# Depthwise products of eight channels at four shifts, side by side in the array

## The chip, the cores and the metric

The kernel runs on one NeuronCore of a Trainium2 chip. The metric is the device time of one execution in microseconds; the median of several runs is compared.

## The reference

The input x is 32 images of 96 channels of 56 x 56 pixels in float32. Two residual layers follow one another, each on a group-normalised copy of its input.

```python
# layer 0: weights and activations quantised to 4 bits
y = act_q(bn1(conv1x1(gn(x), qw(w1))))        # 96 -> 576 channels
y = act_q(bn2(conv3x3_depthwise(y, qw(w2))))  # 576 channels, each alone
x = x + bn3(conv1x1(y, qw(w3)))               # 576 -> 96 channels
# layer 1: three branches of 32 channels, then a 3x3 convolution
n = gn(x)
a = gated_conv3x3(n[:, :32])
b = abs(inverse_fractional_fourier(gated_mix(fractional_fourier(n[:, 32:64]))))
c = inverse_fft(gated_mix(fft(n[:, 64:])))
x = x + conv3x3(concat(a, b, c))
```

## The kernel before

**Layer 0.** The 576 hidden channels are cut into five blocks of 128 (the last has 64). Pixels are handled by parity: u = 0 to 3 numbers the four combinations of odd and even row and column, so an image of a channel is four images of 28 x 28. `expand(b, u)` forms a block's hidden channels at one parity with float matmuls into a pair of PSUM banks (`pe`, L689); `quant_act` (L636, L638) applies scale and ReLU on ScalarE and cuts to 4 bits on VectorE, into `q1s`, whose rows of 872 bytes hold a 28 x 28 image with margins (PQ = 30 bytes a row, QS = 872).

The depthwise convolution needs a channel's four parities in different partitions. The data therefore go through DRAM: `leave(b, u)` writes `q1s` to `sd`, and `enter(b, h)` reads 64 channels back into a tile `d` of two groups, each with 32 channels x 4 parities in the 128 partitions. `depthwise(b, g)` then forms all four output parities of 32 channels at once. A 3 x 3 window on parity images is four shifts (0 or 1 row, 0 or 1 column), so each half image takes four accumulating matmuls of 128 rows by 128 columns, and a group eight, into a PSUM pair `pd` (L723). `quant_act` follows, into `q2s`. There are 18 groups an image. `leave2` and `enter2` take the result through `gd` in DRAM into `q2`, where channels are partitions again, and `project(u)` (`pp`, L748) ends the layer.

**Layer 1.** It has many small steps: transposes (L1031), transforms (L937, L948, L964, L975, L1042), spatial products (`spatial`, L1088), channel mixes in 32-column matmuls of which four write to the four 32-partition strips of one bank (`mix_f`, L1009, and `mix_t`, L1072), and the last 3 x 3 convolution (`final`, L1145), split by a Winograd transform (L1119, L1122). Its tiles have one buffer each. L825 and L843 normalise its input.

**Order.** Three streams (normalising and splitting an image, the rest of layer 0, layer 1) are merged by `arrange`, which also releases the transfers, all issued by SP. Then the class `Order` takes every instruction of the program and plans it anew: `needs` finds what each must wait for, `model` gives each a duration and a lag, `pack` is a list scheduler, run forward and backward eight times, and `hold` fixes the planned order on each engine. The model prices an 8-bit matmul of 392 columns at cols / 2350, that is 0.167 us. It counts no cost for a change of the array's form. Only matmuls with at most 64 input rows are kept together by `group`, which the depthwise ones, with 128 rows, are not.

**Set-up.** The depthwise weights are built on the chip: for each of the 18 groups, VectorE multiplies the quantised taps with a block-diagonal pattern into `dw` (L502).

## Time and profile before

| quantity | value |
|---|---|
| median of 3 runs | 3622.18 us (3622.07 to 3627.27) |
| profiled execution, its own time | 3621.32 us |
| its span, first to last instruction | 3619.5 us |
| granted TensorE clock, mean | 0.947 |
| DMA traffic | 406.08 MB, 491611 packets |

The profile is one execution; the share of an engine's busy time is over the span. The difference of 1.8 us between time and span lies around the first and last instruction. A float32 matmul leaves two records in the trace, an 8-bit one leaves one. Records of matmuls overlap[...], so their mean duration is longer than the distance from one to the next.

### The profile page before, as it was taken

To read this page: it belongs to the slowest core of one execution; us is meant where nothing else is said; L and a number is where in the kernel's file an instruction comes from. 1 tells how busy PE (TensorE), PEld (TensorE's weight loads), DVE (VectorE), ACT (ScalarE), POOL (GpSimd) and SP (SyncE) were. 2 spreads that over 40 slices of the span, in tenths; PEclk is the share of its full clock that TensorE was granted. 3 is DMA by queue.
4 is the path that set the end of the run, shared out by engine and by line. 5 is a ranking of instruction groups with operands and counts; after the bars stand their busy time and mean duration, and the time that the engine had idled before them with its cause. 6 is when DMAs were issued, how large, how long until landed. Compare 5 with 4: busy or idle time off the path is not lost. (4 is left out here: it accounts for less than half of the span.)

```text
span 3619.5 us, 50492 instructions
## 1 busy us (share of the span) xinstructions
PE 3326.5 (92%) x17024; PEld 2059.6 (57%) x17024; DVE 2458.2 (68%) x5553; ACT 2109.3 (58%) x2792; POOL 584.3 (16%) x657
## 2 busy tenths in 40 slices
PE   3799999999999999999999999999999999999987
PEld 2555565556565555565555565555655555655554
DVE  6457676667667667667676766676676676766765
ACT  3566555566556566555566656566555665555542
POOL 3111110111101111101111101111101111101100
PEclk9899999999999999999999999999999999999997
DMA  4344444444454444444444444444444444444332
GB/s 109 103 120 120 113 121 112 108 123 113 116 123 112 106 124 112 115 123 103 108 124 114 118 122 103 114 123 113 117 123 102 118 119 110 124 112 107 101 91 48
DMA packets 491611, 406.08 MB, mean 112 GB/s; under 512 B 221094, under 2 KB 443288, under 8 KB 490328
## 3 DMA queue, kind: packets, MB, share of 16 engines
q1 hardware_dynamic: 487168, 400.10, 44.1%
q10 hardware_dynamic: 4184, 2.75, 0.3%
q8 instruction: 135, 2.21, 0.3%
q14 instruction: 124, 1.02, 0.1%
HBM read 202.71 MB, written 199.97 MB: 111 GB/s over the span
## 5 line engine op out<-in xcount | busy, mean ns | idle before, releaser
L723 PE MATMUL pd<-d,dw 128*128 128x392 fp8e4 x4608 | 1026.7, 358 | 62.8 <-DMA d<-sd 60.3
L636 ACT ACTIVATE q2s<-pd,o,s 128x784 uint8<-128x784 f32 x576 | 578.3, 1004 | 628.8 <-PE pd L723 620.2
L1145 PE MATMUL pc<-V,wcw 96*96 96x392 f32 x2304 | 887.3, 495 | 9.3 <-DVE V L1122 9.3
L636 ACT ACTIVATE q1s<-pe,o,s 128x784 uint8<-128x784 f32 (+1 forms) x640 | 628.9, 1003 | 285.1 <-PE pe L689 283.0
L723 PEld LDWEIGHTS <-dw 128*128 128x128 fp8e4 x4608 | 468.2, 104 | 551.5 <-issue 276.8
L689 PE MATMUL pe<-hi,w1r 96*128 96x392 f32 x1280 | 526.2, 415 | 97.8 <-ACT q1s L636 70.8
L1145 PEld LDWEIGHTS pc<-V,wcw 96*96 96x96 f32 x2304 | 374.7, 164 | 213.6 <-issue 173.2
L689 PE MATMUL pe<-lo,w1r 96*128 96x392 f32 x1280 | 471.1, 368 | 3.3 <-POOL lo L680 2.9
L638 DVE TENSOR_SCALAR q1s<-q1s 128x218 uint32<-128x218 uint32 (+1 forms) x640 | 232.5, 371 | 257.5 <-ACT q1s L636 252.1
L689 PEld LDWEIGHTS pe<-hi,w1r 96*128 96x128 f32 x1280 | 243.0, 192 | 237.9 <-ACT q1s L636 141.0
L638 DVE TENSOR_SCALAR q2s<-q2s 128x196 uint32<-128x196 uint32 x576 | 150.3, 273 | 238.0 <-ACT q2s L636 227.4
L680 POOL TENSOR_TENSOR lo<-v,hi 96x784 fp32r<-96x784 f32 x128 | 238.2, 1861 | 258.0 <-ACT hi L679 241.2
L689 PEld LDWEIGHTS pe<-lo,w1r 96*128 96x128 f32 x1280 | 246.7, 193 | 52.0 <-issue 16.8
L748 PE MATMUL pp<-q,w3q 128*96 128x392 fp8e4 x1280 | 244.0, 333 | 18.9 <-DMA q<-gd 8.3
L628 POOL TENSOR_TENSOR stb<-veb,mhalf 96x1 f32<-96x1 f32 x32 | 23.2, 726 | 1324.2 <-DVE veb L627 1324.2
L748 PEld LDWEIGHTS <-w3q 128*96 128x96 fp8e4 x1280 | 151.1, 124 | 107.5 <-issue 41.5
L679 ACT CAST hi<-v 96x784 fp32r<-96x784 f32 x128 | 107.7, 841 | 174.0 <-DVE v L676 173.3
L758 DVE SCALAR_TENSOR_TENSOR x<-pp,s,x 96x392 f32<-96x392 f32 x256 | 145.4, 617 | 72.9 <-PE pp L748 70.8
L1022 POOL COPY cat<-sq 32x392 f32<-32x392 f32 x256 | 144.9, 566 | 287.2 <-ACT sq L1018 278.7
L1088 PE MATMUL ps<-s,g 128*128 128x392 f32 x512 | 187.7, 502 | 0.0
L1102 ACT ACTIVATE cat<-ps,b 32x392 f32<-32x392 f32 x256 | 162.5, 636 | 16.3 <-PE ps L1088 12.1
L676 DVE TENSOR_SCALAR v<-x,sta 96x784 f32<-96x784 f32 x128 | 89.6, 700 | 101.3 <-POOL lo L680 79.9
(158 smaller groups left out, 4393.5 us busy)
## 6 DMA issues: line engine op xcount, KB each, us to landing
d<-sd SPq DMA_DIRECT2D x288, 218.0 KB
gd<-q2s SPq DMA_DIRECT2D x576, 98.0 KB
sd<-q1s SPq DMA_DIRECT2D x512, 109.0 KB
q<-gd SPq DMA_DIRECT2D x128, 392.0 KB
x<-in_x_dram SPq DMA_DIRECT2D x384, 98.0 KB
out_dram<-x SPq DMA_DIRECT2D x384, 98.0 KB
pd<-pq SPq DMA_DIRECT2D x32, 808.5 KB
F<-pd SPq DMA_DIRECT2D x64, 392.0 KB
```

The lines of the kernel that those rows point to most:

```text
L636: nc.scalar.activation(dst, ps, AF.Relu, bias=offset, scale=scale)
L638: nc.vector.tensor_scalar(w, w, 4, 0x0F0F0F0F, ALU.logical_shift_right, ALU.bitwise_and)
L679: nc.scalar.copy(s["hi"][:, u, :], v)
L680: nc.gpsimd.tensor_tensor(s["lo"][:, u, :], v, s["hi"][:, u, :].bitcast(F32), ALU.subtract)
L689: nc.tensor.matmul(ps[:, half, :HN], w1[:, 128 * b : 128 * (b + 1)], part[:, u, HN * half : HN * (half + 1)], start=(n == 0), stop=(n == 1),)
L723: nc.tensor.matmul(ps[:, half, :HN], dw[n][:, t, :], view(s["d"][b, g], PQ * (14 * half + t // 2) + t % 2, [[PQ, 14], [1, HH]]), start=(t ...
L748: nc.tensor.matmul(ps[:C, half, :HN], w3[:, b * C : (b + 1) * C], q2[b][:, u, HN * half : HN * (half + 1)], start=(b == 0), stop=(b == NB ...
L758: nc.vector.scalar_tensor_tensor(part, src, A3, part, ALU.mult, ALU.add)
L1022: nc.gpsimd.tensor_copy(cat[G : 2 * G, r : r + 7, 1 : 1 + W], src)
L1088: nc.tensor.matmul(ps[:, :HN], s["g0"][:, 128 * t : 128 * (t + 1)], view(s0, PQ * (14 * half + t // 2) + t % 2, [[PQ, 14], [1, HH]]), star ...
L1102: nc.scalar.activation(dst, src, AF.Identity, bias=b0[2 * G : C], scale=1.0)
L1145: nc.tensor.matmul(ps[:C, :HN], wc[:, k, C * dx : C * (dx + 1)], V[:, :, dx : dx + W], start=(dx == 0), stop=(dx == 2),)
```

## The change

The partitions of a depthwise matmul now hold 8 channels x 4 parities x 4 shifts instead of 32 channels x 4 parities. All taps of an output then lie in one matmul of 128 rows by 32 columns, and nothing accumulates. A group of 32 channels is four such sets of 8; set t writes PSUM partitions 32t to 32t + 31. A group still has eight matmuls of 392 columns.

The tile `d` now has each image four times, once for each shift. `enter` issues two DMAs, one for each row shift; each fills every second partition with runs of 6,944 bytes (eight groups of 8 channels in one run), and the two column shifts are source rows that overlap all but one byte. The layouts of `sd` and `gd` in DRAM and the order of channels in the host's constants change to suit. Weights shrink from [128, 4, 128] to [128, 4, 32] a group; `d` grows from [128, 2, 872] in a pool of three buffers to [128, 8, 872] in a new pool, p4, of two. The planner's DMA model is replaced by one that counts packets and run lengths, and a matmul of 32 weight columns is priced at 0.055 us.

```diff
-                        elif pool in ("p1", "p3"):
+                        elif pool in ("p1", "p3", "p4"):
...
-                move = size / 200e3
                 for a in (outs[0], ins[0]):
...
+                    run = min(run, n * size / 16)
+                    n *= size / run
+                    move = max(move, n * 0.0017 if run < 512 else math.ceil(n / 16) * max(0.05 + run / 43e3, run / 27e3))
...
                     took = max(cols / 2350.0, 0.05)
+                    if weights == G and cols >= HN:
+                        took = 0.055
...
-            d = cp.tile([128, 4, 128], FP8, tag=f"dw{g}", name=f"dw{g}")
+            d = cp.tile([128, 4, 32], FP8, tag=f"dw{g}", name=f"dw{g}")
             nc.vector.tensor_tensor(
-                view(d.rearrange("p s m -> p (s m)"), 0, [[128, 4], [4, 32], [1, 4]]),
-                view(w2, 16 * g, [[4, 4], [0, 32], [1, 4]]),
-                view(eye, 0, [[0, 4], [1, 32], [0, 4]]),
+                view(d.rearrange("p s m -> p (s m)"), 0, [[32, 4], [4, 8], [1, 4]]),
+                view(w2, 16 * g, [[4, 4], [0, 8], [1, 4]]),
+                view(eye, 0, [[0, 4], [1, 8], [0, 4]]),
...
+    p4 = Pool(ctx.enter_context(tc.tile_pool(name="p4", bufs=2)), "p4", 2, tiles)
...
-                s["sd", b] = dp.tile([n, 32, 4, QS], FP8, tag=f"sd{n}", name=f"sd{i}_{b}")
+                s["sd", b] = dp.tile([4, 8, 4 * n, QS], FP8, tag=f"sd{n}", name=f"sd{i}_{b}")
             q = q1s[(NB * i + b) % 2]
-            nc.sync.dma_start(out=s["sd", b][:, :, u, :].rearrange("g c n -> c g n"), in_=q[: blk(b), u, :])
+            nc.sync.dma_start(out=s["sd", b][u], in_=q[: blk(b), u, :])
...
-            d = p3.tile([128, 2, QS], FP8, tag="d", name=f"d{i}_{b}_{h}")
-            src = s["sd", b][2 * h : 2 * h + 2].rearrange("g c u n -> (c u) g n")
-            nc.sync.dma_start(out=d, in_=src)
+            d = p4.tile([128, 8, QS], FP8, tag="d", name=f"d{i}_{b}_{h}")
+            n = 8 * QS - 32
+            src = s["sd", b][:, :, 8 * h : 8 * (h + 1), :].rearrange("u c g n -> (u c) (g n)")[:, :n]
+            flat = d.rearrange("p g n -> p (g n)")[:, :n]
+            (pitch, _), row = flat.ap
+            for y in range(2):
+                part = bass.AP(src.tensor, src.offset + PQ * y, [list(src.ap[0]), [1, 2], [1, n]])
+                dst = bass.AP(flat.tensor, flat.offset + pitch * y, [[2 * pitch, 64], list(row)])
+                nc.sync.dma_start(out=dst, in_=part)
             for g in range(2):
-                s["d"][b, 2 * h + g] = d[:, g, :]
+                s["d"][b, 2 * h + g] = d[:, 4 * g : 4 * g + 4, :]
...
                     nc.tensor.matmul(
-                        ps[:, half, :HN],
+                        ps[32 * t : 32 * (t + 1), half, :HN],
                         dw[n][:, t, :],
-                        view(s["d"][b, g], PQ * (14 * half + t // 2) + t % 2, [[PQ, 14], [1, HH]]),
-                        start=(t == 0),
-                        stop=(t == 3),
+                        view(s["d"][b, g][:, t, :], PQ * 14 * half, [[PQ, 14], [1, HH]]),
+                        start=True,
+                        stop=True,
...
-                s["gd", b] = dp.tile([32, n, 4, 2 * HN], FP8, tag=f"gd{n}", name=f"gd{i}_{b}")
-            nc.sync.dma_start(out=s["gd", b][:, g], in_=s["q", b, g])
+                s["gd", b] = dp.tile([n, 32, 4, 2 * HN], FP8, tag=f"gd{n}", name=f"gd{i}_{b}")
+            nc.sync.dma_start(out=s["gd", b][g], in_=s["q", b, g])
```

## The prediction

> **What bounds the kernel now.** I read the page's busy times first, then the busy times of a steady stretch, then the groups of instructions, then the matmuls in order of time, and last the DMA rows.

> ```profile
> PE 3326.5 (92%) x17024; PEld 2059.6 (57%) x17024; DVE 2458.2 (68%) x5553; ACT 2109.3 (58%) x2792; POOL 584.3 (16%) x657
> L723 PE MATMUL pd<-d,dw 128*128 128x392 fp8e4 x4608 | 1026.7, 358 | 62.8 <-DMA d<-sd 60.3
> L636 ACT ACTIVATE q2s<-pd,o,s 128x784 uint8<-128x784 f32 x576 | 578.3, 1004 | 628.8 <-PE pd L723 620.2
> ```

> TensorE is the bound: 92% busy, and the depthwise products (L723) are its largest group. ScalarE, which empties their PSUM, stood idle 620 us waiting for them. The steady stretch says the same more sharply:

> ```profile
> 500.00:3000.00 2500.00, 2356.93 (x12149) 1458.09 (x12148) 1729.20 (x3910) 1504.77 (x1992) 401.81 (x459) 0.95 0.46 116
> ```

> TensorE (first number after the length) 94.3%, VectorE 69%, ScalarE 60%, DMA engines 46%. The period of an image comes from one instruction that runs once in each, layer 1's L843:

> ```profile
> L843 DVE TENSOR_SCALAR torus<-x,stb x32: 1895/1900/1901, 144.3 to 3527.0; 32x3136 f32<-32x3136 f32 x32
> ```

> (3527.0 - 144.3) / 31 = 109.1 us. In it TensorE works 102.9 us, VectorE 75.5, ScalarE 65.7. Now matmuls in order of time (start, us, count):

> ```profile
> 1303.31 0.34 PE L689 MATMUL pe<-hi,w1r 96*128 96x392 f32 x1
> 1303.49 0.34 PE L689 MATMUL pe<-lo,w1r 96*128 96x392 f32 x1
> 1303.76 1.51 PE L1009 MATMUL pz<-F,g 98*32 98x392 f32 x12
> ...
> 3469.92 4.12 PE L1088 MATMUL ps<-s,g 128*128 128x392 f32 x12
> ...
> 3480.39 2.85 PE L1009 MATMUL pz<-F,g 98*32 98x392 f32 x32
> 3484.31 2.92 PE L723 MATMUL pd<-d,dw 128*128 128x392 fp8e4 x16 [1.08 <-DMA d<-sd]
> ```

> Three readings. A depthwise matmul follows the last by (2.92 - 0.34) / 15 = 0.172 us; I use 0.171. The full-width float matmul of 392 columns (L1088) comes every 0.33 us, the 32-column one (L1009), four side by side in 32-row strips of PSUM, every (2.85 - 0.49) / 31 = 0.076: the array already overlaps them fourfold. And entering that form costs: L1009 starts 0.27 us after an L689 that is normally followed after 0.18. Over all such places the trace gives 270 against 176 ns going in, 422 against 328 coming out: **94 ns a switch, 188 ns a visit.**

> ```profile
> q1 hardware_dynamic: 487168, 400.10, 44.1%
> ...
> d<-sd SPq DMA_DIRECT2D x288, 218.0 KB
> ...
> PE pd L723 <- DMA d<-sd: 60.3, 33, 3.2
> ```

> The images come in 288 transfers; one wait an image, 1.8 us on average, reaches TensorE.

> [...]

> **The change, part by part.**

> *Depthwise matmuls.* Removed: 4608 x 0.171 = 788 us of TensorE. Added: the same count, four to a slot of 0.171 if they stand together, and 0.188 for each uninterrupted run of them among full-width work. So run lengths decide. The trace before has 907 runs: 242 single, 259 of two, 89 of three, 57 of four, 88 of five, 30 of six, 97 of sixteen, 32 of thirty-two, 13 others. Three prices:
> - the same runs: each ceil(m/4) x 0.171 + 0.188, together 439 us, saving 349. The runs over eight save 316 of it, the short ones 33: a single costs 0.359 instead of 0.171, a pair is even;
> - the same runs, but no matmul with its weight load under 0.055 (the planner's figure; the smallest ones of the trace, L1031, come every 0.054 to 0.059): 475, saving 313;
> - all in eights: 576 x (0.342 + 0.188) = 305, saving 483.

> I take 400. The planner's ranks space depthwise matmuls closer when each is priced 0.055 instead of 0.167, so more of them fit between two final matmuls (L1145, which stands just before 464 of the 907 runs).

> *Filling.* TensorE then needs 102.9 - 400/32 = 90.4 us an image. At 94.3% that is a period of 95.9. I take 92%, hence 98.3, because a group takes TensorE about 0.5 us and ScalarE still 1.00: while layer 1 waits for its own DMAs, layer 0 now runs at ScalarE's pace and TensorE has gaps. VectorE would be at 77%, ScalarE at 67%; neither sets the end. Gain 31 x 10.8 = 335 us.

> *Images fetched four times.* 288 transfers of 256 packets of 872 bytes become 576 of 64 packets of 6,944. Recorded packets: 872 bytes 51 ns on average, 3,136 194, 7,392 370 (median 285), 12,544 966. The new size by the median 268 ns, by the mean 348, by the slowest row 535. Then 36864 x 0.348 / 16 = 802 us of all 16 engines against 235: DMA share from 44% to (1596 + 567) / 3280 = 66%; ends 61% and 79%. One pair of fetches: 8 packets an engine, 2.8 us instead of 16 x 0.051 = 0.8; ends 2.1 and 4.3. Hidden by the four expands that stand between a block's leaving and its depthwise groups: at least 4 us of ScalarE, usually more. Where that cover is gone, as in the one wait an image above, 2 us more: 31 x 2 = 62 us at worst. I count 0 and keep 62, since the planner knows the longer transfer. Two buffers (p4) instead of three: a fetch must await the groups two fetches back; two groups and four expands lie between, about 6 us of ScalarE[...].

> *SP.* 288 more issues of 0.46 us (median of L714): 4.1 us an image on a queue where leaving and entering transfers stand in order; behind each wait stand the next block's sd and gd. Hidden while SP waits for VectorE (L739 and L708 wait 448 + 407 us for its quantising). Ends 0 and 62 us together with the row above.

> *Building weights.* 18 products of 128x512 at 0.677 us become 128x128, at 0.278 (L542, that shape). This block stands on VectorE just before the first split, which TensorE awaits: 18 x 0.4 = 7 us gained.

> *New order, other DRAM layouts.* Packet counts of sd and gd stay; they count as 0. The planner's other DMA prices reorder everything: images differ by 108.3 to 111.2 us within this run, so plus or minus 1.4 us an image, 45 us.

> Sum against the profiled span: 3619.5 - 335 - 7 = 3277; with 1.8 us around it (3621.3) and the median 0.9 above that, **3280**.

> **Rivals.**
> 1. *Better packing.* All in eights at 94.3%: (102.9 - 15.1) / 0.943 = 93.1; gain 496 + 7, about 3120. For it: TensorE less pressed has less to interleave. Against: ScalarE's pace.
> 2. *Layer 1's own chain, or late images, take back most.* On its last pass alone, layer 1 ran from L825 at 3528.9 to the last final matmul at 3612.3, 83 us, though at a granted clock of 0.81. It can overlap its successor little, since F is reused. With ScalarE and VectorE shared it may need 105: 3490. Two more fetches an image seen at 2.6 us each give about 3440.
> 3. *Scattering, slower than before.* Nothing in the planner keeps eight matmuls together, and it doesn't know the switch. A single costs 0.188 more than now: all single, +866 us, 4490. It decides below a mean run of (0.171 + 0.188) / 0.171 = 2.1; at 1.5 it is 4608/1.5 x 0.359 = 1103, +315, about 3940. For it: 501 of the 907 runs hold one or two. Against: they hold only 760 of 4608 matmuls; the mean is 5.1.
> 4. *The overlap fails for 8-bit operands.* The trace shows it for floats only. Then 788 stay and 0.188 x 907 = 170 come on top, less 7: 3780. A load of the packed form takes 110 ns (98*32), the present 8-bit one 98: no sign of a limit.

> **How the numbers follow.** Forecast 3280, own range 3180 to 3380: 0.52. Rival 1: 0.14. Rival 2: 0.19, nearly all still faster. Rivals 3 and 4: 0.12 together; what is left, 0.03, lies at no change. The range 3100 to 3480 leaves about 2 in 10 out. Faster by over 0.2% (about what a measurement of this kernel can tell from no change) 0.84, within 0.03, slower 0.13.

> **What would show it.** Right: L723 with 32-row tiles starting 7 ns apart in fours, its runs mostly four and more; TensorE busy near 2930 us; a period of 96 to 100; ScalarE near 65%; DMA share 60 to 70%; packets of 6,944 bytes under 0.4 us. Wrong: runs of one and two, gaps of 0.27 before each; PE idle on d<-sd well over 120 us; TensorE below 85% with L843 each time waiting for the previous image's finals.

## The result, and the profile after

The changed kernel takes **3947.21 us** (median of 4 runs, 3936.49 to 3948.6), the kernel before 3622.12 us beside it: a ratio of **1.0891 [1.0866, 1.0915]**, 325 us slower where 342 us faster had been forecast. The profiled execution has a span of 3944.2 us at a granted TensorE clock of 0.853 (before 0.947).

From the page of the changed kernel, the busy times, the granted clock in 40 slices, and the groups of the depthwise matmuls and of their emptying:

```profile
PE 3193.8 (81%) x17024; PEld 1876.9 (48%) x17024; DVE 2378.6 (60%) x5553; ACT 2106.5 (53%) x2792; POOL 563.9 (14%) x657
...
PEclk9888888888888887888888888888888888888888
...
L641 ACT ACTIVATE q2s<-pd,o,s 128x784 uint8<-128x784 f32 x576 | 561.3, 1001 | 422.8 <-PE pd L734 309.4
...
L734 PE MATMUL pd<-d,dw 128*32 128x392 fp8e4 x4608 | 356.4, 377 | 386.3 <-DMA d<-sd 365.4
```

The depthwise group shrank as planned, 1026.7 to 356.4 us, but TensorE as a whole lost only 133 us of busy time and is busy 81% instead of 92%. The clock row hints at where part went: at a lower granted clock the same matmuls last longer (the final ones, `pc`, start 329 ns apart at the full clock and 653 at half of it; on average they last 533 ns instead of 495). And the idle time in front of the depthwise matmuls rose from 62.8 to 386.3 us, nearly all of it for `d<-sd`, the images. The busy times of the steady stretch (length, TensorE, its weight loads, VectorE, ScalarE, POOL, clock, DMA share, GB/s), layer 1's once-an-image instruction, and the three largest waits of TensorE:

```profile
500.00:3000.00 2500.00, 2063.09 (x11106) 1208.06 (x11104) 1532.03 (x3572) 1371.84 (x1818) 358.87 (x420) 0.85 0.55 155
```

```profile
L854 DVE TENSOR_SCALAR torus<-x,stb x32: 1895/1901/1901, 141.0 to 3855.0; 32x3136 f32<-32x3136 f32 x32
```

```profile
PE pd L734 <- DMA d<-sd: 365.4, 85, 8.9
PE pz L1020 <- ACT cat L1093: 62.6, 12, 6.1
PE pz L1020 <- DVE cat L1091: 48.0, 9, 5.8
```

The period is (3855.0 - 141.0) / 31 = 119.8 us against 109.1. The images are late 85 times, by up to 8.9 us. The timeline shows such a place, first the issues on SP's queue, then TensorE's stream (start, us, instruction, in brackets the idle time before it):

```profile
1859.40 0.56 SPq L725 DMA_DIRECT2D d<-sd  x1
...
1862.59 6.25 SPq L453 DMA_DIRECT2D x<-in_x_dram  x12
1868.94 1.85 SPq L725 DMA_DIRECT2D d<-sd  x3
```

```profile
1874.37 0.51 PE L734 MATMUL pd<-d,dw 128*32 128x392 fp8e4 x1 [7.00 <-DMA d<-sd]
...
1874.80 1.83 PE L986 MATMUL pv<-v,e 114*112 114x448 f32 x2
...
1879.15 0.52 PE L734 MATMUL pd<-d,dw 128*32 128x392 fp8e4 x8
```

An image pair is fetched by two DMAs. The first was issued at 1859.40; its second half stands behind twelve loads of a later input and was issued at 1868.94. A depthwise matmul that needs it holds TensorE for 7.00 us, and `pv`, a step of layer 1, stands behind it in the stream. The planner put an instruction in front of data whose transfer it had not yet issued: it did not know that the one needs the other.

The last line shows the packing at work: eight matmuls, two sets of four, in 0.52 us, so (0.52 - 0.35) = 0.17 us from set to set. One set costs what one matmul cost in the kernel before, 0.17 us.

For the accounts below, **own time** of a matmul is the time from its start to the next start on TensorE, at most its duration; the rest is idle. Half-clock time is the sum of the clock records that show half the clock.

| us | before | after |
|---|---|---|
| own time of the depthwise matmuls | 876 | 327 |
| own time of all other matmuls | 2450 | 2867 |
| idle time of TensorE | 266 | 721 |
| of TensorE's time, at the half clock | 385 | 1160 |

The saving of 549 us is there. Against it stand 455 us more idle time and 417 us more own time of the other matmuls, which holds both the slower clock and the changes of the array's form.

### The profile page after: what moved, and what is told of

Same layout as the page of the kernel before. It is cut to its first block, busy times and chain, and to the rows that moved or that the text cites. A ratio compares the mean times of both kernels' runs of the same rounds, so it can differ in the third digit from the quotient of the medians.

```text
span 3944.2 us, 50975 instructions
## 1 busy us (share of the span) xinstructions
PE 3193.8 (81%) x17024; PEld 1876.9 (48%) x17024; DVE 2378.6 (60%) x5553; ACT 2106.5 (53%) x2792; POOL 563.9 (14%) x657
## 3 DMA queue, kind: packets, MB, share of 16 engines
q14 instruction: 126, 1.03, 0.1%
## 5 line engine op out<-in xcount | busy, mean ns | idle before, releaser
L1156 PE MATMUL pc<-V,wcw 96*96 96x392 f32 x2304 | 919.6, 533 | 7.8 <-DVE V L1133 7.8
L641 ACT ACTIVATE q1s<-pe,o,s 128x784 uint8<-128x784 f32 (+1 forms) x640 | 626.5, 1004 | 261.2 <-PE pe L694 255.0
L734 PE MATMUL pd<-d,dw 128*32 128x392 fp8e4 x4608 | 356.4, 377 | 386.3 <-DMA d<-sd 365.4
L694 PE MATMUL pe<-hi,w1r 96*128 96x392 f32 x1280 | 556.4, 435 | 81.0 <-ACT q1s L641 26.7
L734 PEld LDWEIGHTS <-dw 128*32 128x32 fp8e4 x4608 | 100.3, 100 | 660.0 <-issue 381.8
L694 PEld LDWEIGHTS pe<-hi,w1r 96*128 96x128 f32 x1280 | 268.3, 210 | 198.3 <-ACT q1s L641 85.7
L1020 PE MATMUL pz<-F,g 98*32 98x392 f32 x1024 | 181.5, 703 | 162.8 <-ACT cat L1093 62.6
L759 PE MATMUL pp<-q,w3q 128*96 128x392 fp8e4 x1280 | 285.5, 373 | 16.4 <-DMA q<-gd 13.4
L993 DVE COPY pq<-pv 112x448 f32<-112x448 f32 (+1 forms) x160 | 84.4, 528 | 255.2 <-PE pv L986 254.2
L977 ACT COPY v<-pi 114x448 f32<-114x448 f32 (+1 forms) x160 | 76.0, 476 | 284.0 <-PE pi L975 279.6
L643 DVE TENSOR_SCALAR q1s<-q1s 128x218 uint32<-128x218 uint32 (+1 forms) x640 | 160.1, 270 | 88.7 <-ACT q1s L641 79.7
```

The costliest lines, as they stand in the source:

```text
L641: nc.scalar.activation(dst, ps, AF.Relu, bias=offset, scale=scale)
L643: nc.vector.tensor_scalar(w, w, 4, 0x0F0F0F0F, ALU.logical_shift_right, ALU.bitwise_and)
L694: nc.tensor.matmul(ps[:, half, :HN], w1[:, 128 * b : 128 * (b + 1)], part[:, u, HN * half : HN * (half + 1)], start=(n == 0), stop=(n == 1),)
L734: nc.tensor.matmul(ps[32 * t : 32 * (t + 1), half, :HN], dw[n][:, t, :], view(s["d"][b, g][:, t, :], PQ * 14 * half, [[PQ, 14], [1, HH]]), ...
L759: nc.tensor.matmul(ps[:C, half, :HN], w3[:, b * C : (b + 1) * C], q2[b][:, u, HN * half : HN * (half + 1)], start=(b == 0), stop=(b == NB ...
L993: nc.vector.tensor_copy(dst, src)
```

## The experiments

**1. Is the second fetch unseen? Is it mispriced?** `needs` takes the partition step of an access to be the tile's row pitch. The second fetch writes every second partition, so its step is twice that; its box came out as partitions 0 to 64 at a place beyond the row's end, and met no read of `d`. `e_seen` mends the box; `e_price` also gives the fetch its length; `e_drain` adds to `e_price` 94 ns for each change of the array's form in the list scheduler, and prices a depthwise matmul at 0.045 instead of 0.055 us.

```diff
+                    if m in tiles and tiles[m][0] == "p4":
+                        n, pitch = (n - 1) * (pitch // (8 * QS)) + 1, 8 * QS
```

> The changed kernel, with one thing added: the planner's dependence search now takes the step of a DMA's partition dimension into account, so that it sees that the depthwise matmuls read what the second fetch (row shift 1, every second partition from the first on) writes. In the changed kernel it does not, and may put that fetch behind anything. Theory A (the loss comes from the unseen fetch: TensorE waits in a fixed order for images whose second half stands behind twelve loads of x): TensorE's idle time on d<-sd falls from 365 us to under 120, the granted clock rises from 0.85 to above 0.90, the time falls below the kernel before, to 3300 +- 100. Theory B (the fetches are too large, and late whatever the order): the idle time on d<-sd stays above 300 us and the time within 3 percent of the changed kernel's, 3830 to 3950. Theory C (layer 1's own chain of steps, once depthwise work no longer fills its waits, sets the period together with the halved clock): the wait on d<-sd goes, but waits inside layer 1 take its place; 3600 to 3800.

Measured: 3692.91 us, 1.0193 [1.0161, 1.0225]. With nothing but the planner's sight mended, 254 of the 325 us are gone. Its largest waits on TensorE:

```profile
PE pp L761 <- DMA q<-gd: 149.5, 31, 6.0
PE pd L736 <- DMA d<-sd: 134.1, 81, 8.0
```

The wait for images fell from 365.4 to 134.1 us. Theory B is out. Theory A's figures were not reached (a wait under 120 us, a clock above 0.90 where 0.872 was granted, some 3300 us); the time lies in theory C's range.

```diff
+                if self.tiles.get(outs[0].tensor.name) == "p4":
+                    move = 1.41
...
+                    lag += 0.5
```

> As e_seen, and the planner is told what a fetch really takes: 1.41 us of the engines for each of the two (4 packets of 0.353 us an engine, the mean recorded) instead of 1.03, and 0.5 us more lag. Theory A: little left to gain, 0 to 2 percent against e_seen (waits on d<-sd under 60 us). Theory B: a large part of its waits is mispricing, so 3 to 8 percent against e_seen. Theory C: no gain, within 1 percent of e_seen.

Measured: 3629.34 us, 1.0024 [1.0011, 1.0038]. The wait for images is down to 31.7 us:

```profile
PE pd L740 <- DMA d<-sd: 31.7, 13, 7.7
```

So the planner's blindness and the short price together are 318 us: that is the loss, shown. But what remains is only the kernel before again; a saving of 543 us of own time on the depthwise matmuls (876 to 333) is still missing.

```diff
+                t += 0.094 * (self.narrow[k] != form)
+                form = self.narrow[k]
```

> As e_price, and the planner adds 0.094 us whenever TensorE goes from full-width to 32-column matmuls or back, and prices a depthwise matmul 0.045 us. If the switches matter as the prediction priced them, the depthwise runs become longer than 9.6 on average, TensorE loses 20 to 60 us less to switches, and the time falls by 0.5 to 2 percent against e_price. If layer 1's chain is the bound (theory C), nothing changes within 1 percent.

Measured: 3698.85 us, 1.0223 [1.0195, 1.0252], a miss. There were 459 runs instead of 493, and more idle time (500 against 440 us). Plans made under slightly different prices can differ by about 2%, here 70 us; a difference of that size between two plans is no proof of anything. By this measure the 254 us of `e_seen` stand, and the 64 us from `e_seen` to `e_price` alone do not.

**2. Where did TensorE's saving go?** In every kernel here that is not overlapped as in experiment 4, layer 1's norm into `F` starts 0.0 to 1.7 us after the last final matmul of the image before, for all but the first and the last two images. So layer 1 is a serial chain from image to image. `e_cut_before` and `e_cut_price` take a wait out of it:

```diff
+            pds[i] = s["pd"]
...
-                src = s["pd"][H * q : H * (q + 1)]
+                src = pds[max(i - 1, 0)][H * q : H * (q + 1)]
```

> The kernel before, with one wait of layer 1's chain taken out: the images of the fractional Fourier branch that an image fetches back through device memory are those of the image before it, so the fetch has not to wait for this image's leave. Instructions and bytes are the same; the output is not the reference's, since that branch of each image comes from the image before. Theory P (before is bound by TensorE, 93% busy with the order's small losses): little can be gained, 3560 to 3640 us. Theory C (the chain of layer 1 sets the period in both kernels): the chain is shorter by the round trip, about 5 to 8 us of an image, and 31 images bring 3380 to 3470 us if TensorE has the room; with 2991 us of TensorE's own work and its refill at the start, C too can give no less than some 3300.

> The same wait taken out of e_price (the changed kernel with a planner that sees the second fetch and its length). The output is again not the reference's for the same reason. Theory C: TensorE has 440 us of idle time and runs 900 us at the half clock while it waits for the chain, so a shorter chain must bring more here than in the kernel before: 3350 to 3480 us, a gain of 150 to 280 us, with less time at the half clock. Theory B (the fetches' traffic slows everything, whatever the chain): the gain is no larger than in e_cut_before, and the time stays above 3550 us.

Measured: 3619.9 us (1.0002 [0.9993, 1.001]) and 3707.6 us (1.0238 [1.0221, 1.0255]). In `e_cut_price` the cut did not do what it was for: the planner let `pz`, the first step after the removed wait, start 50.6 us after the norm, where it had been 49.5, so that run decides nothing. In `e_cut_before` it did: `pz` starts 40.3 us after the norm instead of 45.8, and still the time is the same, as theory P said. In the kernel before, a shorter chain alone brings nothing; the table under experiment 3 shows what took its place. `e_repeat` issues each set of four three times over:

```diff
-            for half in range(2):
+            for half in (0, 0, 0, 1, 1, 1):
```

> e_price with each set of four depthwise matmuls issued three times over (same result, 9,216 more matmuls in sets of four). If TensorE's work were what bounds e_price, 2 x 1152 more sets at 166 ns would bring 380 us: 3900 us or more. Theory C: the chain of layer 1 has slack in which TensorE is idle or at the half clock, the added work falls into it and brings the clock back: 3600 to 3720 us, half-clock time down from 901 us to below 600, granted clock from 0.876 to 0.92 or more.

Measured: 4052.11 us, 1.1196 [1.1172, 1.1221]. I had expected the work to fall into slack; it did not: 425 us of own time more cost 423 us. Theory C, as I had put it, was wrong in this. Again the table under experiment 3 shows why.

**3. The two halves of the change apart.** `e_taps` is the kernel before with less depthwise work and nothing else. `e_old`, `e_pack`, `e_fetch` and `e_price` are a square: old or packed matmuls, one fetch or four, all under the same DMA prices.

```diff
 e_taps, in depthwise
-                for t in range(4):
+                for t in range(1):
...
-                        start=(t == 0),
-                        stop=(t == 3),
+                        start=True,
+                        stop=True,
```

> The kernel before with one of the four shifts of each depthwise product left out of four kept: 1,152 matmuls in place of 4,608, all else unchanged (three taps in four are missing from the result). TensorE loses 3,456 x 0.171 = 591 us of work at the full clock, about what the packing saves, but with no change of the array's form, no second fetch and no more DMA traffic. Theory F (the products were only filler: layer 1's chain and ScalarE's pace set the period, and TensorE slows its clock when it has less to do): 3550 to 3650 us, half-clock time up from 385 to 800 us or more. Theory B (the saving is worth its time and the fourfold fetches eat it): 3200 to 3350 us. Theory S (the array's changes of form eat it): also 3200 to 3350 us.

```diff
 e_pack, against e_price
-            d = p4.tile([128, 8, QS], FP8, tag="d", name=f"d{i}_{b}_{h}")
+            d = p3.tile([128, 2, QS], FP8, tag="d", name=f"d{i}_{b}_{h}")
...
-                        view(s["d"][b, g][:, t, :], PQ * 14 * half, [[PQ, 14], [1, HH]]),
+                        view(s["d"][b, g], PQ * (14 * half + t // 2) + t % 2, [[PQ, 14], [1, HH]]),
```

> e_price with the fetches of the kernel before: images fetched once, three buffers of 128 x 2 x 872 bytes, and the four matmuls of a set read the same image at four offsets (the matmuls, their form and their number are the changed kernel's; each output gets the right weights on the wrong channels). Theory F: 3550 to 3650 us. Theory B: 3200 to 3350 us. Theory S: 3550 to 3650 us, with e_taps at 3350 or less.

```diff
 e_old, against before: the model of DMACopy
-                move = size / 200e3
...
+                    move = max(move, n * 0.0017 if run < 512 else math.ceil(n / 16) * max(0.05 + run / 43e3, run / 27e3))
```

> The kernel before with nothing but the changed kernel's prices of DMA transfers in its planner. All theories: 3560 to 3680 us; it is the reference for e_pack and e_fetch, whose planner has these prices too.

```diff
 e_fetch, against e_price
-                        ps[32 * t : 32 * (t + 1), half, :HN],
-                        dw[n][:, t, :],
+                        ps[:, half, :HN],
+                        dw[n % 3][:, t, :],
...
-                        start=True,
-                        stop=True,
+                        start=(t == 0),
+                        stop=(t == 3),
```

> e_price with the old matmuls (128 x 128, four accumulating), but with the images fetched four times, seen by the planner at their length (only 3 of the 18 weight tiles are kept for room, so the values are not the reference's). TensorE's work is that of the kernel before. Theory F: the fetches are hidden once the planner sees them, so 3600 to 3720 us. Theory B: the fetches cost some 300 us whatever the matmuls are: 3850 us or more. Theory S: 3600 to 3700 us.

| measured, us (ratio to before) | one fetch | four fetches, seen and priced |
|---|---|---|
| old matmuls | e_old 3609.86 (0.9975 [0.9964, 0.9985]) | e_fetch 3845.24 (1.0615 [1.059, 1.064]) |
| packed matmuls | e_pack 3530.27 (0.9744 [0.9709, 0.9779]) | e_price 3629.34 (1.0024 [1.0011, 1.0038]) |

`e_taps`: 3554.88 us, 0.9818 [0.9798, 0.9837]. Theory F, the products as filler, was nearest for `e_taps` (in its range, with 745 us at the half clock where 800 were forecast) and for `e_pack` (20 us under its range), and too low by 125 us for `e_fetch`, where theory B's figure was met but for 5 us. Theory S is out: it put `e_taps`, which has no added change of form, at 3350 us or less.

Every step between these kernels is one plan against another, so the 70 us by which plans can differ must be kept in mind. **Less depthwise work is worth little by itself**: 63 us without any side effect of the packing (`e_taps`), 80 with it (`e_pack`), where theory B's 3200 to 3350 us asked for some 300. **The fetches cost something even when the planner knows them**: 235 us beside the old matmuls, which is clear, and 99 beside the packed ones, which is little more than the scatter. Whether they cost less beside packed matmuls is not shown. From the kernel before to the changed one the steps are - 8 (DMA prices), - 80 (packing), + 99 (fetches) and + 318 (not seen, underpriced); they add up to 3946 because each starts where the last one ends, so the sum tests nothing.

What became of 600 us in `e_taps`? Its busy times, two waits, and the place where one image's layer 1 hands over to the next:

```profile
PE 2980.9 (84%) x13568; PEld 1853.5 (52%) x13568; DVE 2405.9 (68%) x5553; ACT 2090.6 (59%) x2792; POOL 590.8 (17%) x657
...
PEclk9898989899999899989998998988898988999887
```

```profile
PE pd L723 <- DMA d<-sd: 125.0, 35, 5.7
PE pp L748 <- DMA q<-gd: 115.6, 49, 5.0
```

```profile
1865.73 0.82 PE L1145 MATMUL pc<-V,wcw 96*96 96x392 f32 x2
...
1866.90 1.90 DVE L825 TENSOR_SCALAR F<-x,stb 32x3136 f32<-32x3136 f32 x1
```

No engine is full by its busy time. The last final matmuls of one image end at 1866.55, the norm of the next starts at 1866.90. From the traces, means over images 4 to 27, with the chain cut in two at the first final matmul:

| us | norm to first `pc` | first `pc` to last `pc` | period | half clock, whole run |
|---|---|---|---|---|
| before | 68.4 | 40.9 | 109.4 | 385 |
| before, the last image, alone | 56.0 | 27.3 | | |
| e_cut_before | 62.0 | 46.7 | 109.2 | 194 |
| e_old | 73.0 | 36.0 | 109.1 | 116 |
| e_taps | 71.7 | 35.2 | 107.3 | 745 |
| e_pack | 69.5 | 37.0 | 107.1 | 966 |
| e_price | 68.4 | 40.5 | 108.9 | 901 |
| e_repeat | 67.4 | 57.6 | 125.0 | 812 |
| e_fetch | 65.0 | 50.7 | 116.3 | 516 |
| after | 77.9 | 42.0 | 119.9 | 1160 |

The second part is full of TensorE work, the final matmuls with layer 0's products between them: in the kernel before, `e_old`, `e_cut_before` and `e_taps` TensorE has no idle time in it. The first part is a string of small transforms, copies and two round trips through device memory. How the image divides into the two says little by itself: before, `e_old` and `e_cut_before` have the same matmuls, and their first parts differ by 11 us, their second parts by nearly as much the other way. What stays is the sum, 107 to 109 us, whether the depthwise products take 27 us of own time an image (before) or 8 (`e_taps`).

Three rows show how. In `e_cut_before` the first part is 6.4 us shorter, and 16.3 us of depthwise own time stand in the second part instead of 10.6: what the chain gave, the full part took. In `e_taps` the products had been the filler of the first part: without them TensorE idles 15.0 us in it instead of 6.4, and runs at the half clock for 17.2 us instead of 10.5. In `e_repeat` most of the added work lies in the second part (16.1 us of depthwise own time, in `e_price` 5.8), which grows by 17.1 us. So in the kernel before, layer 1's chain and TensorE's work in it stand at about the same length, and less of one alone brings little. Alone, the last image takes 83 us; the other 26 appear only beside layer 0's work, and no run separates which engine they come from. The changed kernel loses in the first part, where the late images hold up `pv` and `pz`; `e_fetch` in the second.

**4. Let the images of layer 1 overlap.** If the serial chain holds the period, starting the next image's statistics, norm and gates during the last convolution must pay where TensorE has room. `V` of the convolution's second half moves from `F`'s buffer into that of `u`, the stream no longer holds the norm back for the last final step, and six steps move ahead of the final ones in the stream:

```diff
-                s["V", half] = p1.tile([C, 6, 7 * (W + 2)], F32, tag=("torus", "F")[half], name=f"V{i}_{half}")
+                s["V", half] = p1.tile([C, 6, 7 * (W + 2)], F32, tag=("torus", "u")[half], name=f"V{i}_{half}")
...
-            S(norm, K("norm"), {K("second"): 1.2, (i - 1, 1, "c", 1, 5): 0.0} if i else {K("second"): 1.2}, dve=1.9),
+            S(norm, K("norm"), {K("second"): 1.2}, dve=1.9),
...
+    early = ('first', 'second', 'norm', 'hidden', 'row', 'gates')
...
+            at = len(rest) - 12
+            rest[at:at] = first
```

(18 instead of 12 in `e_hoist_price`, 6 in `e_hoist_old`; no run shows what the other depths give.)

> e_taps (three taps in four left out, as there) with the first steps of layer 1 (statistics, norm into F, gates, and so the round trip xd to xh) issued ahead of the last convolution of the image before, and V of that convolution's second half in another buffer than F, so that they can overlap. Theory C (layer 1's serial chain sets the period where TensorE has room): the 13.5 us from norm to the first transform leave the chain of each image, less what other stages give back; 3554 becomes 3250 to 3420 us. Theory P (the order of the engines' streams sets the period, not the chain): 3500 to 3600 us.

> The same overlap in e_price (same computation as the changed kernel). Theory C: 3629 becomes 3380 to 3530 us. Theory P: 3570 to 3680 us.

> The same overlap in the kernel before (same computation). TensorE's own work is 3326 us of which 385 at the half clock, so some 3130 us at the full clock: at the 92 to 94% that the prediction read, a floor near 3400. Theory C (the chain holds this kernel too): 3450 to 3550 us. If TensorE alone bounds it: 3580 to 3640 us.

> The same overlap in e_old (the kernel before with the changed DMA prices; same computation). Theory C: 3420 to 3540 us. If TensorE alone bounds it: 3570 to 3630 us. It is also the candidate to beat both kernels.

| us (ratio to before) | serial | overlapped |
|---|---|---|
| three taps in four left out | 3554.88 | 3327.06 (0.9195 [0.918, 0.9211]) |
| changed kernel, fetch seen and priced | 3629.34 | **3478.5 (0.9625 [0.9596, 0.9654])** |
| before with the new DMA prices | 3609.86 | 3539.41 (0.9788 [0.9772, 0.9804]) |
| before | 3618.13 | 3696.87 (1.0213 [1.0198, 1.0228]) |

In `e_hoist_taps`, with the very same matmuls as `e_taps`, the busy times and the clock, the norm of an image, a final matmul of the image before that comes 46 us later, and the period's instruction:

```profile
PE 2834.9 (85%) x13568; PEld 1746.6 (53%) x13568; DVE 2403.7 (72%) x5553; ACT 2101.1 (63%) x2792; POOL 583.5 (18%) x657
...
PEclk9689899999998999999999999999999999998888
```

```profile
1722.83 1.90 DVE L825 TENSOR_SCALAR F<-x,stb 32x3136 f32<-32x3136 f32 x1
...
1768.90 0.82 PE L1145 MATMUL pc<-V,wcw 96*96 96x392 f32 x2
```

```profile
L843 DVE TENSOR_SCALAR torus<-x,stb x32: 1894/1896/1897, 140.7 to 3232.8; 32x3136 f32<-32x3136 f32 x32
```

Nothing of the work changed; the period fell to (3232.8 - 140.7) / 31 = 99.7 us and 228 us are gained, three times what two plans differ by. **Layer 1's serial chain set the period where TensorE had room**; theory P is out for these kernels. In `e_price` the overlap brings 151 us, in theory C's range. In `e_old` it brings 70, just inside that range but no more than the scatter of plans; TensorE is 94% busy in `e_hoist_old`, so little room is left. The buffer and the order changed together, and neither was tried alone.

`e_hoist_before` missed both expectations, 79 us slower. Its trace has 744 us at the half clock (before 385) and more loads of ScalarE's function tables, here the row of the square root:

```profile
L1018 ACT ACT_TABLE_LOAD x62 | 79.5, 1283 | 1.1
```

The kernel before has 32 of these, and 60 loads fewer in all, that is 77 us of ScalarE. In this plan 62 of the 64 square roots have a load, and so have 30 of the 32 gates at L885, which have none in the kernel before. No run took its causes apart.

The packed kernel with the overlap, 3478.5 us, is the fastest here that computes the reference. It is 61 us ahead of `e_hoist_old`, no more than two plans can differ by, so that the packing is what puts it ahead is not shown. What is clear of the scatter: once images overlap, less depthwise work pays. Leaving out three taps in four brings 63 us without the overlap, and with it `e_hoist_taps` is 212 us ahead of `e_hoist_old` (whose DMA prices and depth of overlap differ).

## Why the prediction was wrong

Forecast and result are 667 us apart. By the experiments some 417 of them belong to the fetches (318 + 99) and some 255 to the forecast that less TensorE work is less time (335 forecast, 80 found).

**The step "Images fetched four times" failed first.** It counted 0 and kept 62 us, "since the planner knows the longer transfer". It did not: the dependence was not seen at all (254 us, after to `e_seen`), and the model's price was short as well, 1.03 us for a fetch that takes an estimated 1.41, four packets an engine of 353 ns on average (64 us, `e_seen` to `e_price`, within the scatter of plans). With both mended, 99 us of the fetches remain. I had read how `needs` is called, not what its box becomes for a partition step of two pitches; the diff had that step in it. The sizes of the same step held: a packet of 6,944 bytes took 353 ns on average (median 264), forecast 348; together 812 us of 16 engines, forecast 802. Half of the rows start one byte off, and the packets' times do not fall into two halves for it: 72% of all of them took 261 to 264 ns.

**The step "Filling" failed second, and would have failed alone.** It turned 12.5 us less TensorE work an image into 10.8 us less period, on the reading that TensorE is the bound and stays 92% full. `e_pack`, with the work gone and no extra fetch, gained 80 us, not 335. TensorE was 92% busy, and still not the only bound: layer 1's chain, with its waits for engines that it shares with layer 0, already took the whole 109 us of an image. The overlap, which leaves TensorE's work as it is and takes 228 us off `e_taps`, shows it. The one number that could have told me was in the trace: each image's norm starts when the last final matmul before it ends. I took the last image's 83 us alone for the chain's length, and placed the risk in rival 2.

**The step "Depthwise matmuls" held.** Own time fell by 549 us; 481 runs, of 9.6 on average, replaced 907 of 5.1. The changes of form cost about what was forecast for them, 94 ns: at the full clock a depthwise matmul starts 421 ns after a final one instead of 329, and a final one 260 ns after a depthwise one instead of 165 to 177. The first of the two falls into the other matmuls' own time, an estimated 44 us for 481 runs, so that some 505 us are net, 400 forecast. The overlap that the trace before showed for floats, matmuls of a set 6 to 7 ns apart, holds for 8-bit operands too: the four start 3 to 4 ns apart, and a set comes every 0.17 us. So rival 4 is out, and rival 3 as well: its 3940 us came out within 7 us, but by luck, since its mechanism, runs shorter than 2.1, is absent.

**Rival 2 was right in kind**, layer 1's chain and late images. Its figures, 3490 and 3440, were too low: late images cost 365 us on TensorE, not 2.6 us twice an image, and the chain alone gave back less than it assumed: `e_pack` has a period of 107.1 us, where the rival put 105.

**Building weights** shrank by the 7 us forecast (18 products of 277 ns instead of 677), but the block starts 3.0 us later, and layer 1's first once-an-image instruction runs 3.3 us earlier (141.0 instead of 144.3). The new DMA prices, counted as plus or minus 45, gave 8 in `e_old`; the 108.3 to 111.2 us behind that figure hold for the middle of the run, and some images at its ends lie outside. SP's issues were not tried alone.

Of the signs named in advance, four sets in 0.17 us, long runs and packets under 0.4 us came; TensorE near 2930, a period of 96 to 100, ScalarE near 65% and a DMA share of 60 to 70% did not (3193.8, 119.8, 53%, 53%). Of the signs of failure TensorE's idle time on `d<-sd` (365.4 us) and TensorE below 85%, with each norm waiting for the previous image's finals, came; the runs of one and two did not (49 of 481).

## What to carry to other kernels

An engine that is 92% busy is not the only bound if a serial chain of the same length runs beside it: less of either alone brings little. Look for the place where one iteration's first instruction starts as the last one's final instruction ends, and ask what else would let it start earlier. When an operation changes shape, look whether whatever orders the program still sees its reads and writes: a dependence that the planner misses is still waited for when the program runs (7.00 us in the place shown above), so nothing breaks, and the time is lost in waits. And when a planner makes the order, learn first by how much two of its plans differ, before a small gain is given a cause.

## What I had not expected of the hardware

Taking work away from TensorE raised the half-clock time from 385 to 745 us (`e_taps` beside the kernel before) and from 116 to 966 us (`e_pack` beside `e_old`). What this costs was not isolated. It can be little: with the same matmuls, `e_old` has 269 us less of it than the kernel before and is 8 us faster.

**Fetches that are seen, priced and hardly waited for still cost.** In `e_fetch` TensorE waits 22.7 us for images, but 96.3 in 26 waits for `F<-pd`, for which it waits once, 5.4 us, in the kernel before:

```profile
PE pz L1026 <- DMA F<-pd: 96.3, 26, 5.0
...
PE pd L740 <- DMA d<-sd: 22.7, 11, 7.8
```

These waits are not where the time goes: they lie in the first part of an image, which is 8.0 us shorter than in `e_old`, its counterpart with one fetch, and `e_hoist_taps`, with one fetch and the lowest time of all, has 70.0 us of them. The second part is 14.7 us longer, and 15.9 us of depthwise own time stand in it instead of 7.6: with four fetches the plan puts more of these products where TensorE has hardly any idle time. TensorE's other matmuls take 155 us more own time, with 516 us at the half clock instead of 116. Whether the bytes, the two buffers or the issues bring the plan to this, no run tells.
